# Two graph attention layers on one core: three of eight layer 0 tiles fetched by indirect DMAs, and GpSimd's once-a-batch work in pieces

## The chip, the core and the metric

The kernel runs on one core of a Trainium2 chip. The core has five engines with an instruction stream each: PE (TensorE, matrix products and transposes; PEld is its weight load), DVE (VectorE), ACT (ScalarE), POOL (GpSimd) and SP (SyncE, which here only issues DMAs). The engines wait for each other through semaphores, and each works through its own stream in order. The metric is the device time of one execution, in microseconds; lower is better.

## The reference, cut to what matters

There are B = 16 graphs ("batches") of N = 1024 nodes with D = 64 numbers each. `adj` is a 1024 x 1024 matrix of zeros and ones, symmetric, with ones on the diagonal; a row has about nine ones.

```python
# layer 0: attention with 8 heads over the neighbours
scores = einsum('bmhd,bnhd->bhmn', q, k) * scale + edge_bias[edges]
scores = where(edges > 0, leaky_relu(scores, 0.2), -1e9)
out = einsum('bhmn,bnhd->bmhd', softmax(scores), v) @ Wp + bp
x = layernorm(x + out)
# layer 1: one head, additive scores
s = leaky_relu(u[:, :, None, :] + v[:, None, :, :], 0.2)
e = where(adj > 0, einsum('bijf,f->bij', s, a), -9e15)
x = layernorm(x + elu(einsum('bij,bjf->bif', softmax(e), hp)))
```

## The kernel before, in words

The adjacency is sparse, so the kernel never forms all pairs. For every group of 8 neighbouring rows (`GR`) it makes a list of `SLOTS` = 120 columns: 112 places for nodes that some row of the group has an edge to, and the 8 rows themselves. A mask then removes the pairs without an edge.

A batch is cut into 8 tiles (`NT`) of 128 rows, 16 groups each. What happens to a tile of layer 0 is spread over four steps:

- `load` (SP) brings the tile's column numbers (`cb`, 544 KB, the same on all partitions) from a small DRAM tensor `col_d`, and `indicate` (DVE, L475) compares them with the partition's own number in two operations: the result `f` is a matrix of zeros and ones that picks columns.
- `gather` (PE, L499) multiplies `f` with x to bring the 112 node vectors of each group together. To keep float32 precision x is split into three bfloat16 parts (`thirds`, five operations on POOL, once a batch and layer). A tile costs 2 x 26 matmuls, in two halves `hs`; ACT copies each half out of PSUM into `xg` (L505). `own` (POOL, L484) adds the group's own 8 rows.
- `queries` (PE L586, DVE L587), `score` (PE L603, DVE L611 to L620), `exps` (ACT L629), `divide` (DVE L636, then POOL L637, once for each half of the heads), `turn` (eight transposes of `xg`, PE L518, ACT L519, giving `xn` with a node on each partition), `turn_weights` (PE L645), `attend` (PE L655), `heads`, `rows`, `residual`.
- At the end of a batch of layer 0, `Norm.scale` (POOL L549 to L552: add, pow, subtract, multiply, on all 8 tiles at once) gives x1. Layer 1 (`project`, `weigh`, `exps`, `attend`, `end`) then takes the same tiles with its own gathers; `own_rows` (POOL L728) makes one of its operands, `sums` (L721, L723) another.

Beside this DVE makes the lists of the next batch (`prepare`: it reads `adj`, packs and sorts; its column numbers are `win`, its row bits `who`), cut by `yield` into 41 pieces (`PIECES`).

The order of all instructions on all engines is written out by hand. One loop runs over steps g; step g takes tile t = g mod 8 of batch b = g div 8. In one step the loop calls the stages of several tiles: `gather` and `queries` of layer 0 tile g, `score` of g-1, `exps`, `divide` and `attend` of g-2, `heads` to `residual` of g-3, and of layer 1 the tiles that lie `LAG` = 12 steps back. Five times a step `Lists.place` puts in pieces of `prepare` (as many as `QUOTA` gives to that step) and at most one piece of a side list (the end of layer 1, the last part of the lists). All steps of layers 0 and 1 are thereby interleaved, so that one engine's wait is another tile's work. Buffers rotate in pools: a tile with `bufs=3` can be written again when its third successor needs it and its last reader is done.

The code leaves indirect DMAs unused: every DMA is issued by SP.

Of the kernel before, what the change touches and what calls it, by code (L numbers as in the profile page):

```python
# [9 lines left out]
F32 = mybir.dt.float32  # L10
# [23 lines left out]
def kernel(  # L34
# [30 lines left out]
    def sub(n):  # L65
        return slice(n * D, n * D + D)
# [172 lines left out]
    root = fst.tile([P, 1], F32, name="root")  # L239
    nc.vector.memset(root, -0.5)  # L240
    setup.close()

# [11 lines left out]
    KEPT = 40  # L254
    PIECES = 41
    MULT = 4
# [24 lines left out]

    started, edges, masks, late = {}, {}, {}, {}

    def start(b):

        xs = dbl.tile([P, NT, D], F32, tag="xs", bufs=3, name=f"xs_{b}")
        dg = sml.tile([P, NT], I32, tag="dg", bufs=2, name=f"dg_{b}")
        diag = adj[b].rearrange("r c -> (r c)")[0 : N * N : N + 1]
        for n in range(2):
            nc.sync.dma_start(xs[sub(n), :, :], by_rows(x[b], n))  # L290
            nc.sync.dma_start(
                dg[sub(n), :], diag[n * 512 : n * 512 + 512].rearrange("(t r) -> r t", r=D)
            )
        ads = {}

        def load(k):
            hs, T = divmod(k, NT)
            if hs < 2:
                ads[k] = dbl.tile([P, 2, SEG], I32, tag="ad", bufs=4, name=f"ad_{b}_{hs}_{T}")
                nc.sync.dma_start(  # L300
                    ads[k], adj[b, ts(T, P), :].rearrange("p (n c) -> p n c", n=2)[:, :, hs * SEG : hs * SEG + SEG]
                )

        for k in range(4):
            load(k)
        started[b] = xs, dg, ads, load

    def prepare(b):

        if b not in started:  # L310
            start(b)
        xs, dg, ads, load = started.pop(b)
        flags = sml.tile([P, 32], F32, tag="flags", bufs=2, name=f"flags_{b}")
# [95 lines left out]
        yield  # L409

        rows_s = per.tile([P, NT, 2 * CAP2], BF16, tag="rows_s", name=f"rows_s_{b}")
        for n in range(2):
            for q in range(NQ):
# [5 lines left out]
                )  # L419
        edges[b] = (xs, col_d)  # L420
        late[b] = (flags, dg, rows_s)

    def finish(b):

        flags, dg, rows_s = late.pop(b)
        mask = dbl.tile([P, NT, SLOTS], BF16, tag="mask", bufs=4, name=f"mask_{b}")
        nc.vector.tensor_scalar(mask[:, :, 0 : 2 * CAP2], rows_s, code, NEG, ALU.not_equal, ALU.mult)
# [17 lines left out]
    def thirds(src, tag, nm):  # L445

        t3 = dbl.tile([P, 3, NT, D], BF16, tag=tag, bufs=3, name=f"{tag}_{nm}")
        rest = src
        less = per.tile([P, NT, D], F32, tag="less", name=f"less_{tag}_{nm}")
        for k in range(3):  # L450
            nc.gpsimd.tensor_copy(t3[:, k, :, :], rest)
            if k < 2:
                nc.gpsimd.tensor_tensor(less, rest, t3[:, k, :, :], ALU.subtract)
                rest = less
        return t3

    class Tiles:


        def load(self, t):  # L460
            nm = f"{self.b}_{self.layer}_{t}"
            self.cb[t] = cb = dbl.tile([P, NSEG, 2, NQ, WIN], BF16, tag="cb", bufs=3, name=f"cb_{nm}")
            nc.sync.dma_start(
                cb.rearrange("p s n q k -> p (s n q k)"),
                self.col_d[t].rearrange("s n q k -> (s n q k)").unsqueeze(0).to_broadcast([P, NSEG * 2 * NQ * WIN]),
            )
# [54 lines left out]
        def begin(self, x_):  # L521

            b = self.b
            px = ps_g.tile([P, 512], F32, tag="g", name=f"px{self.layer}_{b}")
            columns_T(px, x_)
            self.xT = dbl.tile([P, 512], F32, tag=f"xT{self.layer}", name=f"xT{self.layer}_{b}")
            nc.scalar.copy(self.xT, px)
            self.t3 = thirds(x_, "x3", f"{self.layer}_{b}")
            self.f, self.xg, self.xn = {}, {}, {}

    def banks(tag, name):
# [3 lines left out]
    class Norm:  # L535
# [10 lines left out]

        def scale(self, dst, y):
            rs = sml.tile([P, NT], F32, tag="rs", name=f"rs_{self.nm}")
            nc.gpsimd.tensor_tensor(rs, self.mv[:, :, 1], eps.to_broadcast([P, NT]), ALU.add)  # L549
            nc.gpsimd.tensor_tensor(rs, rs, root.to_broadcast([P, NT]), ALU.pow)  # L550
            nc.gpsimd.tensor_tensor(dst, y, self.mv[:, :, 0:1].to_broadcast([P, NT, D]), ALU.subtract)
            nc.gpsimd.tensor_tensor(dst, dst, rs.unsqueeze(2).to_broadcast([P, NT, D]), ALU.mult)  # L552

    class Layer0(Tiles):
        layer = 0

        def __init__(self, b):
            self.b, self.cb, (self.xs, self.col_d) = b, {}, edges[b]
            self.begin(self.xs)
            self.mx = dbl.tile([P, 2, NG // 4], F32, tag="mx", name=f"mx_{b}")  # L560
            self.y = dbl.tile([P, NT, D], F32, tag="y", name=f"y0_{b}")
            self.norm = Norm(f"0_{b}")
            self.qp, self.ls, self.den, self.w = {}, {}, {}, {}

        def constants(self):
# [124 lines left out]
        def residual(self, t):  # L690
            if t % 2 == 0:
                return
            nc.vector.tensor_tensor(self.y[:, t - 1 : t + 1, :], self.pr, self.xs[:, t - 1 : t + 1, :], ALU.add)
            for t_ in (t - 1, t):
                self.norm.look(self.y, t_)

        def end(self):
            x1 = dbl.tile([P, NT, D], F32, tag="x1", name=f"x1_{self.b}")
            self.norm.scale(x1, self.y)

# [3 lines left out]
            nc.vector.tensor_tensor(bad, bad, low, ALU.max)  # L704
            return x1

    class Layer1(Tiles):
        layer = 1

        def __init__(self, b, x1):  # L710
            self.b, self.cb, self.x1, (_, self.col_d) = b, {}, x1, edges[b]
            self.begin(x1)
# [4 lines left out]
        def sums(self):  # L717
            pu = ps_g.tile([P, NT, D], F32, tag="g", name=f"pu_{self.b}")
            for t in range(NT):
                for n in range(2):  # L720
                    nc.tensor.matmul(pu[sub(n), t, :], self.xT[:, ts(t, D)], w1h[:, n, :], start=True, stop=True)  # L721
            self.u = dbl.tile([P, NT, D], F32, tag="u", name=f"u_{self.b}")
            nc.vector.tensor_tensor(self.u, pu, rows_b[:, 0:1, :].to_broadcast([P, NT, D]), ALU.add)  # L723
# [85 lines left out]
        def end(self):  # L809
# [12 lines left out]
            norm = Norm(f"1_{b}")  # L822
            for t in range(0, NT, 2):
                norm.look(y, t)
                norm.look(y, t + 1)
                yield
            norm.scale(o, y)
            yield
            for n in range(2):
# [7 lines left out]
    PLACES = 5  # L837
    QUOTA = (3, 3, 5, 6, 6, 6, 6, 6)
    l0, l1 = {}, {}
# [6 lines left out]
    class Lists:  # L846


        def __init__(self):
# [6 lines left out]
            self.done, self.part, self.side = 0, None, []  # L856

        def place(self, g, k):
            b, t = divmod(g + AHEAD, NT)
            due = PIECES * b + sum(QUOTA[:t]) + QUOTA[t] * (k + 1) // PLACES  # L860
            last = k == PLACES - 1
            while self.done < due and self.part != ("keys" if last else "sums"):
                self.part = next(self.work, None)
                self.done += 1
# [7 lines left out]
    with tc.manual_schedule(engines={getattr(mybir.EngineType, e) for e in order}):  # L872
        for _ in prepare(0):
            pass
        for _ in finish(0):
            pass
        l0[0] = Layer0(0)
        l0[0].constants()
        l0[0].load(0)
# [3 lines left out]
        for g in range(NT * B + LAG + 7):  # L883
            u = g - LAG
            b, t = divmod(g, NT)
            if t == 0 and 0 < b < B:
                lists.side.append(finish(b))
            lists.place(g, 0)
            at(l0, g - 2, "exps", 0, range(4))
            at(l0, g - 1, "score", lambda: at(l0, g - 2, "divide", 0))  # L890
            if (g - 1) // NT not in l0:
                at(l0, g - 2, "divide", 0)
            at(l0, g - 2, "exps", 1, range(2))
            at(l0, g, "gather", 0)
            at(l0, g - 3, "heads")
            at(l0, g, "gather", 1)
            at(l0, g - 2, "exps", 1, range(2, 4))
            back = ps_z.tile([P, 3, D], F32, tag="e", name=f"back_{g}") if g > 3 else None
            at(l1, u - 3, "rows", back)
            at(l0, g - 3, "rows", back)  # L900
            at(l0, g, "queries")
            at(l1, u - 3, "residual")
            at(l0, g - 3, "residual")
            if t == 6 and b - 2 in l1:
                lists.side.append(l1[b - 2].end())
            at(l0, g - 2, "divide", 1)
            at(l1, u - 1, "project")
            lists.place(g, 1)
            at(l1, u, "gather", 0)
            at(l0, g - 1, "turn")  # L910
            lists.place(g, 2)
            at(l1, u - 1, "weigh")
            at(l1, u - 1, "exps")
            at(l0, g + 1, "indicate")
            at(l0, g + 2, "load")
            at(l1, u, "gather", 1)
            if t == 2 and b - 1 in l0:
# [19 lines left out]
            if t == 3 and b - 1 in l1:  # L937
                l1[b - 1].sums()
            if t == NT - AHEAD and b + 1 < B:
                l0[b + 1] = Layer0(b + 1)  # L940
                l0[b + 1].load(0)
# [415 lines left out]
```

## Time and profile before

| | us |
|---|---|
| median of three timed runs | 2500.33 (2499.95 to 2503.71) |
| the profiled execution | 2508.74 |
| its span in the profile | 2506.8 |
| busy: PE, DVE, ACT, POOL | 2308.1, 2012.1, 1445.2, 912.9 |
| one batch in the middle (1210.40 to 1356.03) | 145.63 |
| granted clock, mean of the span | 0.988 |

A profile page gives, for each engine, the time in which it worked on some instruction. Groups of instructions are named by line, engine, operation, the tile written and the tiles read, then the shapes, the number, the busy time and the mean of one in ns, and the idle time ahead of them with what ended it. Matmuls overlap in the array, so the busy time of a group is less than number times mean. A table of stretches gives the length and each engine's busy time with its number of instructions, the granted clock, the share of the DMA engines and GB/s. The timeline merges neighbouring instructions of a kind into one row: start, duration, engine, line.

### The profile page before, as it was taken

The numbers are of one execution on the slowest core, as the hardware profiler recorded it, in microseconds if no ns is written. First come the engines' busy times: TensorE is split into PE (matmuls) and PEld (weight loads), VectorE is DVE, ScalarE is ACT, GpSimd is POOL, SyncE is SP. The second block draws the span as 40 slices with busy tenths as digits, with TensorE's granted clock in tenths as the row PEclk, the third lists the DMA queues.
The fourth block names the chain that finished last, engine by engine and source line by source line (L and its number), as shares of the span: only waits on it lengthen the run. The fifth ranks groups of instructions, "written<-read, shape, count | busy, mean of one in ns | idle before, by whom it ended". The sixth has DMA issues, their size and how long they took to land. (4 is left out here: it accounts for less than half of the span.)

```text
span 2506.8 us, 110853 instructions
## 1 busy us (share of the span) xinstructions
PE 2308.1 (92%) x48706; PEld 1957.7 (78%) x48706; DVE 2012.1 (80%) x5237; ACT 1445.2 (58%) x4401; POOL 912.9 (36%) x1106
## 2 busy tenths in 40 slices
PE   5387999999999999999999999999999999999986
PEld 3376788878788887878788787888878888888864
DVE  6687879888888988888898888889888888876642
ACT  0154656656565665656566566656656665666743
POOL 1133333434334343433434343342434434243331
PEclk9998999999999999999999999999999999999998
DMA  3412332423233242323324232332423233221210
GB/s 102 122 59 89 104 103 78 133 77 116 73 102 108 78 133 80 114 73 107 103 78 133 84 109 75 106 103 78 133 86 108 81 100 106 62 92 57 66 52 18
DMA packets 190543, 230.66 MB, mean 92 GB/s; under 512 B 91492, under 2 KB 157092, under 8 KB 190052
## 3 DMA queue, kind: packets, MB, share of 16 engines
q1 hardware_dynamic: 190052, 223.49, 28.3%
q8 instruction: 384, 6.29, 1.0%
q14 instruction: 107, 0.88, 0.1%
HBM read 218.23 MB, written 5.21 MB: 89 GB/s over the span
## 5 line engine op out<-in xcount | busy, mean ns | idle before, releaser
L499 PE MATMUL pg<-f,x 128*64 128x272 bf16 (+2 forms) x13312 | 804.5, 272 | 37.4 <-DVE f L475 34.5
L499 PEld LDWEIGHTS <-x 128*64 128x64 bf16 x13312 | 662.0, 109 | 115.5 <-issue 70.4
L637 POOL TENSOR_TENSOR ls<-ls,den 128x480 f32<-128x480 f32 x256 | 285.8, 1117 | 921.1 <-DVE den L636 912.6
L475 DVE TENSOR_SCALAR f<-cb,jrow 128x2176 bf16<-128x2176 bf16 x512 | 491.6, 1001 | 0.3 <-DMA cb<-col_d 0.3
L505 ACT COPY xg<-pg 128x448 f32<-128x448 f32 x512 | 271.5, 530 | 356.1 <-PE pg L499 355.1
L629 ACT ACTIVATE ls<-ls,mx 128x120 f32<-128x120 f32 x1024 | 391.2, 386 | 4.8 <-DVE mx L620 4.8
L519 ACT COPY xn<-pt 120x512 f32<-120x512 f32 x512 | 277.3, 597 | 11.8 <-PE pt L518 7.1
L751 ACT ACTIVATE r<-pz 128x480 f32<-128x480 f32 x256 | 132.1, 568 | 247.0 <-PE pz L746 247.0
L518 PE MATMUL pt<-ident,xg 128*120 128x128 f32 x2048 | 273.9, 276 | 0.0
L484 POOL COPY xg<-xT 128x64 f32<-128x64 f32 x256 | 107.2, 426 | 387.9 <-PE pt L518 345.4
L518 PEld LDWEIGHTS pt<-ident,xg 128*120 128x120 f32 x2048 | 224.0, 137 | 27.3 <-issue 24.8
L752 DVE SCALAR_TENSOR_TENSOR r<-pz,r 128x480 f32<-128x480 f32 x256 | 155.4, 649 | 50.6 <-ACT r L751 50.6
L629 ACT ACTIVATION_READ_ACCUMULATOR ls<-ls,mx 128x1 f32 x1024 | 194.8, 190 | 0.0
L619 DVE SCALAR_TENSOR_TENSOR ls<-sc 128x480 f32<-128x480 f32 x256 | 191.5, 748 | 0.0
L620 DVE TENSOR_REDUCE mx<-ls 128x4 f32<-128x480 f32 x256 | 167.2, 653 | 8.8
L611 DVE TENSOR_TENSOR sc<-s,rowc 128x480 f32<-128x480 f32 x256 | 155.1, 647 | 22.7 <-PE s L603 21.0
L746 PEld LDWEIGHTS pz<-rw,ub 64*64 64x64 f32 x4096 | 122.6, 133 | 63.9 <-issue 58.5
L655 PE MATMUL z<-w,xn 120*64 120x64 f32 x4096 | 159.2, 227 | 4.4 <-ACT w L647 4.4
L587 DVE TENSOR_TENSOR qp<-pq,qb 128x512 f32<-128x512 f32 x128 | 87.9, 686 | 90.0 <-PE pq L586 89.8
L655 PEld LDWEIGHTS z<-w,xn 120*64 120x64 f32 x4096 | 138.4, 139 | 27.7 <-ACT w L647 19.4
L645 PE MATMUL pp<-ident,ls 128*120 128x128 f32 x1024 | 142.0, 280 | 19.3 <-POOL ls L637 16.6
L740 PE MATMUL pz<-xg,w2d 64*64 64x480 f32 x1024 | 140.4, 588 | 17.1 <-DVE sc L611 17.1
(212 smaller groups left out, 3881.1 us busy)
## 6 DMA issues: line engine op xcount, KB each, us to landing
cb<-col_d SPq DMA_DIRECT2D x256, 544.0 KB
ad<-in_adj_dram SPq DMA_DIRECT2D x256, 256.0 KB
xs<-in_x_dram SPq DMA_DIRECT2D x32, 128.0 KB
rows_s<-slot_d SPq DMA_DIRECT2D x256, 14.0 KB
out_dram<-o SPq DMA_DIRECT2D x32, 128.0 KB
col_d<-col SPq DMA_DIRECT2D x128, 4.2 KB
dg<-in_adj_dram SPq DMA_DIRECT2D x32, 2.0 KB
slot_d<-slot SPq DMA_DIRECT2D x16, 28.0 KB
```

The source lines that it names most:

```text
L475: nc.vector.tensor_scalar(fj.rearrange("p s n q k -> p (s n q k)"), cb.rearrange("p s n q k -> p (s n q k)"), jrow[:, j : j + 1], None, AL ...
L499: nc.tensor.matmul(pg[sub(n), :, FIRST * a_ + lo : FIRST * a_ + to], self.t3[:, k, 4 * hs + 2 * a_ + j, :], f[j][:, 2 * hs + a_, n, :, lo:to],
L505: nc.scalar.copy(dst, pg)
L518: nc.tensor.transpose(pt[:, q, :], xg[:, 4 * m + q, :], ident)
L519: nc.scalar.copy(self.xn[t][:, ts(m, 4), :], pt)
L611: nc.vector.tensor_tensor(sc, both[n], self.rowc[:, n, ts_].unsqueeze(2).to_broadcast([P, 4, SLOTS]), ALU.add)
L619: nc.vector.scalar_tensor_tensor(ls, scs[n], SLOPE, scs[n], ALU.mult, ALU.max)
L620: nc.vector.tensor_reduce(self.mx[:, n, ts_], ls, XX, ALU.max, negate=True)
L629: nc.scalar.activation(ls[:, q, :], ls[:, q, :], AF.Exp, bias=neg[:, q : q + 1], accum_out=den[:, q : q + 1])
L637: nc.gpsimd.tensor_tensor(ls, ls, den.unsqueeze(2).to_broadcast([P, 4, SLOTS]), ALU.mult)
L655: nc.tensor.matmul(zz[sub(n), q, :], xn[:, q, sub(n)], w_[n][:, q // 2, sub(q % 2)], start=True, stop=True)
L752: nc.vector.scalar_tensor_tensor(r, pz[n], SLOPE / (1.0 - SLOPE), r, ALU.mult, ALU.add)
```

## The change

For tiles 2, 5 and 7 of every batch of layer 0, the 120 node vectors of each group are fetched from DRAM by indirect DMAs issued by POOL. `prepare` makes their row numbers (`at_d`: one column of 120 numbers for each group; number 0 is an empty place), `start` makes a copy of x in DRAM in the groups' numbering (`table`). One DMA brings one group (120 rows of 256 bytes, a row on each partition) into `xf`; a tile takes 16, a batch 48. They arrive with a node on each partition, which is what `attend` reads as `xn`; for `xg` the tile is transposed on PE by eight transposes in `gather`, and `turn` does nothing for it. Such a tile has no `load`, `indicate` or `own`. `place` issues one or two fetches each time, two steps ahead of the batch that they are for.

POOL's once-a-batch work is cut up: `thirds` yields after each operation, and the norms of both layers work on two tiles at a time, in place for layer 0 (`x1` is now `y`). The next batch's `Layer0` is made at step 4 in place of 6. Within a step that has a fetched tile the order differs: both halves of its `gather` first, `queries` ahead of `heads`, the second half's last exponentials and the `rows` after the layer 1 gather. In those steps and in the ones after them (`soon`) layer 1's second gather half stands ahead of `weigh`. In the norms the four operations are as before, on [P, 2] and [P, 2, D]. The pieces are now 43, at most two a place, with 7 as the last two entries of `QUOTA`; some pools have one buffer less or more.

```diff
+    own_at = fst.tile([P, GR], F32, name="own_at")
...
+    seg_at = fst.tile([P, N // SEG], F32, name="seg_at")
...
-    PIECES = 41
+    PIECES = 43
...
     def start(b):
         xs = dbl.tile([P, NT, D], F32, tag="xs", bufs=3, name=f"xs_{b}")
+        table = dram.tile([N + 1, D], F32, tag="table", bufs=3, name=f"table_{b}")
+        nc.sync.dma_start(table[0:1, :], x[b, 0:1, :])
...
         for n in range(2):
             nc.sync.dma_start(xs[sub(n), :, :], by_rows(x[b], n))
+            nc.sync.dma_start(
+                table[1 : N + 1, :].rearrange("(t n r) d -> n t r d", n=2, r=D)[n],
+                x[b, n * 512 : n * 512 + 512, :].rearrange("(t r) d -> t r d", r=D),
+            )
...
     def prepare(b):
...
+        tb = per.tile([P, NSEG, WIN], F32, tag="tb", name=f"tb_{b}")
+        nc.vector.tensor_tensor(tb, seg_at.unsqueeze(2).to_broadcast([P, NSEG, WIN]), win, ALU.subtract)
+        nc.vector.scalar_tensor_tensor(tb, who, 0.5, tb, ALU.is_ge, ALU.mult)
+        tv = tb.rearrange("p (s a) k -> p s a k", a=2)
+        at_s = per.tile([P, SLOTS], F32, tag="at_s", name=f"at_s_{b}")
+        av = at_s[:, 0 : 2 * CAP2].rearrange("p (s k) -> p s k", k=CAP2)
+        nc.vector.tensor_copy(av[:, :, 0:FIRST], tv[:, :, 0, 0:FIRST])
+        nc.vector.tensor_tensor(av[:, :, FIRST:WIN], tv[:, :, 0, FIRST:WIN], tv[:, :, 1, 0:SHARE], ALU.max)
+        nc.vector.tensor_copy(av[:, :, WIN:CAP2], tv[:, :, 1, SHARE:WIN])
+        nc.vector.tensor_copy(at_s[:, 2 * CAP2 : SLOTS], own_at)
+        yield
...
+        yield "sums"
+        pi = ps_z.tile([SLOTS, P], F32, tag="z", name=f"pi_{b}")
+        nc.tensor.transpose(pi, at_s, ident)
+        at_d = dbl.tile([SLOTS, P], I32, tag="at_d", name=f"at_d_{b}")
+        nc.vector.tensor_scalar(at_d, pi, 0.0, float(N), ALU.max, ALU.min)
+        edges[b] = (col_d, table, at_d)
...
     def thirds(src, tag, nm):
-        for k in range(3):
-            nc.gpsimd.tensor_copy(t3[:, k, :, :], rest)
-            if k < 2:
-                nc.gpsimd.tensor_tensor(less, rest, t3[:, k, :, :], ALU.subtract)
-                rest = less
-        return t3
+        def parts(rest):
+            for k in range(3):
+                nc.gpsimd.tensor_copy(t3[:, k, :, :], rest)
+                yield
+                if k < 2:
+                    nc.gpsimd.tensor_tensor(less, rest, t3[:, k, :, :], ALU.subtract)
+                    rest = less
+                    yield
+        return t3, parts(src)
...
-            self.xT = dbl.tile([P, 512], F32, tag=f"xT{self.layer}", name=f"xT{self.layer}_{b}")
+            self.xT = dbl.tile([P, 512], F32, tag=f"xT{self.layer}", bufs=2 - self.layer, name=f"xT{self.layer}_{b}")
...
-            self.t3 = thirds(x_, "x3", f"{self.layer}_{b}")
+            self.t3, parts = thirds(x_, "x3", f"{self.layer}_{b}")
+            lists.side.insert(0, parts)
...
-        def scale(self, dst, y):
+        def scale(self, dst, y, t):
+            two = slice(t - 1, t + 1)
+            for t_ in (t - 1, t):
+                self.look(y, t_)
...
+    def fetch(b, t, k):
+        _, table, rows_at = edges[b]
+        if k == 0:
+            fetched[b, t] = dbl.tile([SLOTS, NQ, P], F32, tag="xf", bufs=3, name=f"xf_{b}_{t}")
+        n, q = divmod(k, NQ)
+        g = D * n + NQ * t + q
+        nc.gpsimd.indirect_dma_start(
+            out=fetched[b, t][:, q, sub(n)], out_offset=None, in_=table[:, :],
+            in_offset=bass.IndirectOffsetOnAxis(ap=rows_at[:, g : g + 1], axis=0),
+        )
...
     class Layer0(Tiles):
+        def gather(self, t, hs):
+            if t not in FETCHED:
+                return super().gather(t, hs)
+            nm = f"{self.b}_{t}"
+            if hs == 0:
+                self.xn[t] = fetched.pop((self.b, t))
+                self.xg[t] = dbl.tile([P, NQ, SLOTS], F32, tag="xg0", bufs=2, name=f"xgf_{nm}")
+            pt = ps_p.tile([P, 4, SLOTS], F32, tag="p", name=f"ptf_{nm}_{hs}")
+            for q in range(4):
+                nc.tensor.transpose(pt[:, q, :], self.xn[t][:, 4 * hs + q, :], ident[0:SLOTS, 0:SLOTS])
+            nc.scalar.copy(self.xg[t][:, ts(hs, 4), :], pt)
...
         def residual(self, t):
...
-            for t_ in (t - 1, t):
-                self.norm.look(self.y, t_)
+            self.norm.scale(self.y, self.y, t)
...
-            self.u = dbl.tile([P, NT, D], F32, tag="u", name=f"u_{self.b}")
+            self.u = dbl.tile([P, NT, D], F32, tag="u", bufs=1, name=f"u_{self.b}")
...
-    QUOTA = (3, 3, 5, 6, 6, 6, 6, 6)
+    QUOTA = (3, 3, 5, 6, 6, 6, 7, 7)
+    FETCHED = (2, 5, 7)
...
+        def fetches(self, g, k):
+            b, t = divmod(g + AHEAD, NT)
+            i, todo = PLACES * t + k, 2 * NQ * len(FETCHED)
+            for j in range(todo * i // (PLACES * NT), todo * (i + 1) // (PLACES * NT)):
+                if b < B:
+                    fetch(b, FETCHED[j // (2 * NQ)], j % (2 * NQ))
         def place(self, g, k):
+            self.fetches(g, k)
...
-            while self.done < due and self.part != ("keys" if last else "sums"):
+            end = self.done + 2 if (t, k) != (NT - 1, PLACES - 1) else due
+            while self.done < min(due, end) and self.part != ("keys" if last else "sums"):
...
+        for k in range(2 * PLACES):
+            lists.fetches(k // PLACES - AHEAD, k % PLACES)
         l0[0] = Layer0(0)
+        for _ in lists.side.pop():
+            pass
...
+            if t in FETCHED:
+                at(l0, g, "gather", 0)
+                at(l0, g, "gather", 1)
+                at(l0, g - 2, "exps", 1, range(2))
+                at(l1, u - 3, "rows", back)
+                at(l0, g, "queries")
+                at(l0, g - 3, "heads")
...
+            if t in FETCHED:
+                lists.place(g, 1)
+                at(l1, u, "gather", 0)
+                at(l0, g - 2, "exps", 1, range(2, 4))
+                at(l0, g - 3, "rows", back)
...
+            soon = t in FETCHED or (g - 1) % NT in FETCHED
+            if soon:
+                at(l1, u, "gather", 1)
...
+            if t == 4 and b + 1 < B:
+                l0[b + 1] = Layer0(b + 1)
             if t == NT - AHEAD and b + 1 < B:
-                l0[b + 1] = Layer0(b + 1)
                 l0[b + 1].load(0)
```

## The prediction

> **What bounds the kernel now.** I read the page's busy times first, then the stretch between successive query additions (DVE L587), which cuts one batch into its eight steps, then the timeline inside two steps.
>
> ```profile
> span 2506.8 us, 110853 instructions
> PE 2308.1 (92%) x48706; PEld 1957.7 (78%) x48706; DVE 2012.1 (80%) x5237; ACT 1445.2 (58%) x4401; POOL 912.9 (36%) x1106
> ```
>
> PE is the busiest engine and POOL the idlest. The table by step (start:end, length, then PE, PEld, DVE, ACT and POOL busy, clock, DMA share) says the same of one batch:
>
> ```profile
> 1227.64:1247.03 19.39, 18.24 (x377) 15.04 (x373) 13.03 (x34) 11.48 (x35) 5.14 (x7) 1.00 0.21 70
> 1247.03:1268.87 21.84, 19.91 (x423) 16.92 (x425) 20.71 (x54) 11.77 (x37) 12.79 (x14) 1.00 0.16 53
> 1286.41:1302.71 16.30, 16.30 (x346) 13.94 (x350) 15.16 (x38) 10.87 (x34) 3.71 (x5) 1.00 0.20 73
> 1318.92:1337.63 18.71, 18.19 (x407) 15.67 (x409) 16.61 (x39) 11.77 (x36) 11.22 (x14) 1.00 0.46 140
> 1210.40:1356.03 145.63, 140.41 (x3036) 119.96 (x3040) 124.94 (x314) 90.22 (x276) 56.85 (x68) 1.00 0.31 99
> ```
>
> A batch takes 145.63 us; PE works 140.41 of it and stands 5.2. The second row is the exception: there DVE has 20.71 of 21.84 us, and POOL its longest burst. These rows are the ends of tiles 1, 2, 4 and 6 with the starts of the next. DMA engines are busy a third of the time and bound nothing.
>
> **What is removed.** A fetched tile has no gather of 52 matmuls (L499) and no two indicator rows on DVE (L475).
>
> ```profile
> 1215.22 1.58 PE L499 MATMUL pg<-f,x 128*64 128x272 bf16 x26
> 1216.73 1.09 PE L645 MATMUL pp<-ident,ls 128*120 128x128 f32 x8
> L475 DVE TENSOR_SCALAR f<-cb,jrow 128x2176 bf16<-128x2176 bf16 x512 | 491.6, 1001 | 0.3 <-DMA cb<-col_d 0.3
> ```
>
> Half a gather keeps PE from 1215.22 to 1216.73, 1.51 us, so a tile 3.02 us and a batch, with three tiles, 9.06 us. The eight transposes of turn (L518) are not saved: a fetched tile needs eight in the other direction, of the same size but for 120 columns in place of 128; I cost that at nothing. DVE loses 6 x 1.0 = 6.0 us a batch. ACT loses two copies a tile (L505, 530 ns; the other two stay), POOL three small copies (L484, 426 ns), SP three loads of 544 KB; none of these is on the path. PE gets one transpose a batch (pi), 0.29 us by L780's 285 ns. DVE gets seven small operations (tb, at_s, at_d), about 7 x 0.23 = 1.6 us by L390 to L406. Both removals of tile 2 lie in the first row above, of tile 5 in the third, of tile 7 in the fourth; the second row gains nothing. With the same 5.2 us of standing, a batch would be 145.63 - 9.06 + 0.29 = 136.9 us.
>
> **What is added on POOL.** A tile needs 16 indirect DMAs of 120 rows, so a batch 48, six a step. The trace has no such instruction. Lowest row: an ordinary issue on SP, about 0.6 us (L300, two in 1.27). Highest: POOL's dearest operation, 1862 ns (L550, pow). I take 1.2, the middle, since POOL's full-width operations (L637, 1117 ns) lie there too. That is 57.6 us, with 28.8 and 89.4 as ends.
>
> The layer norms go from two calls of four operations a batch to eight calls on a quarter of the data. A call was 0.20 + 1.69 + 1.05 + 1.25 = 4.2 us. Now the pow has 2 elements in place of 8: at least 0.42 and at most 1.69, I take 0.57 (0.2 fixed, the rest in proportion). The two wide ones go to 128x128, for which L327 has 0.54 us. A call is 1.85, eight are 14.8 against 8.4: +6.4 us (ends +5 and +15). Thirds is the same five operations, put in pieces. POOL outside the DMAs is then 56.85 + 6.4 - 1.3 = 62 us, and in all 62 + 57.6 = 119.6 of 136.9 us, 87%. It still fits; what of it is late is seen below.
>
> **What the added POOL work does to DVE.** The same trace shows POOL and DVE disturbing each other. POOL works without a pause from 1250.26 to 1261.65, and DVE meanwhile does this:
>
> ```profile
> 1250.54 1.68 POOL L550 TENSOR_TENSOR rs<-rs,root 128x8 f32<-128x8 f32 x1
> 1260.66 0.99 POOL L451 CAST x<-less_x 128x512 bf16<-128x512 f32 x1
> 1252.41 0.93 DVE L367 SCALAR_TENSOR_TENSOR kb<-left,c 128x32 f32<-128x32 int32 x1
> 1253.45 2.24 DVE L475 TENSOR_SCALAR f<-cb,jrow 128x2176 bf16<-128x2176 bf16 x2
> 1257.63 1.02 DVE L364 TENSOR_SCALAR left<-left 128x32 int32<-128x32 int32 x1
> 1259.48 2.74 DVE L475 TENSOR_SCALAR f<-cb,jrow 128x2176 bf16<-128x2176 bf16 x2
> 1273.05 1.48 DVE L475 TENSOR_SCALAR f<-cb,jrow 128x2176 bf16<-128x2176 bf16 x2
> ```
>
> A pair of indicators takes 1.48 us alone and 2.24 and 2.74 beside POOL; operations of 0.19 us take 0.93 and 1.02. The excess in that burst is 0.74 + 0.76 + 0.28 + 0.84 + 0.46 + 1.26 = 4.3 us in 11.4, or 0.38 us of DVE per us of POOL. If an indirect DMA holds DVE up like a cast, 57.6 + 5.1 = 62.7 added us cost DVE 24 us, and DVE has 124.9 - 6.0 + 1.6 + 24 = 144.5: as long as a batch is now. If it holds DVE up not at all, DVE has 120.5 plus 2 for the norms. The truth of an operation that reads no wide tile is likely below half: I take a third for the fetches, 7 us, and the 2 of the norms, hence DVE 130 us, below PE's 136.9 in the sum, but not step by step: the second row keeps its 20.7 us, and the rows where the quotas rise get up to two pieces (about 1 us) more. I add 3.6 us a batch for steps that DVE or a late POOL then ends (ends 0 and 8.7), which makes 140.5.
>
> The Trainium skill, "SBUF — State Buffer", sections "A bandwidth-pool intuition that's wrong (but worth ruling out)" and "Who interferes with whom", speaks against this change: VectorE and GpSimd share one port pair as an exclusive lock, and a DMA whose descriptors GpSimd writes took about 620 ns alone and 3100 ns beside a VectorE copy. By 3.1 us a fetch POOL would need 62 + 149 = 211 us a batch, an estimate of some 3,500 us in all; by 0.62 us it would be hidden. The stretched rows above agree that the two engines exclude each other, but nothing here shows an issue from GpSimd.
>
> **The new waits.** The first fetch of a batch waits for at_d, which DVE writes last in the step before; behind it on POOL stands the first division (L637), needed about 12 us later by PE. Once a batch, perhaps 2 us, hidden. Each later fetch waits for the landing of the eighth before it, over 20 us earlier: nothing. The fetches end over a step before the tile is used (tile 7, the closest: issued up to step 5, used in step 7), so PE does not wait for data. The tables (two DRAM copies and a row a batch) stand on SP's queue before the ad loads; three cb issues go, so the queue is no longer. With one buffer for xT1 and u, ACT's copy and DVE's addition wait for POOL's last reader in the same step: at most one POOL operation, about 1 us a batch, inside the 3.6. The division of the second half (L637) moves later in a fetched step; about 6 us of PE work (project, gather, weigh) still lies between it and its transpose.
>
> **Head.** Before the first gather POOL now runs 12 fetches, which wait for at_d at about 79 us (slots are done at 76.56, plus 2), then the thirds that ran at 53.84: 79 + 14.4 + 4.4 = 98 us against the gather's 94.2. With the tables' traffic about +6 us (0 to +12).
>
> **Sum.** Batch 0 has no layer 1 beside it and PE is not the bound there, so fifteen batches count: 15 x (145.63 - 140.5) = 77 us, less 6: 71. The profiled execution, 2508.74 us (span 2506.8, 1.9 around it), becomes 2438. The three timed runs have a median of 2500.33, 8.4 below; I take the change off that: **about 2430 us**.
>
> **Rivals.** (1) *All of PE's gain stays:* fetches do not disturb DVE. 15 x 8.7 = 131, less 2: 2370 us. For it: DVE's sum falls by 4 us. Against: DVE's 20.71 of 21.84 us. Chance 0.12. (2) *DVE eats the gain:* a fetch disturbs it like a cast, DVE has 144.5 us and a batch 144.5 to 147; 2490 to 2525. Chance 0.14. (3) *POOL becomes the bound* (slower): POOL's 62 + 48c passes today's 145.63 us once a fetch costs c = 1.74 us. At 1.86 it is 151.3 us, 15 x 5.7 + 12 = +97, about 2600 us; each further 0.1 us adds 72. Before that point PE already waits for divisions, since POOL is in order. For it: pow costs 1.86 and every fetch may wait for a 0.78 us indicator. Against: 1.2 is the middle. Chance 0.28. (4) That the gathers don't go is excluded: 2,496 matmuls leave the instruction stream.
>
> **How the numbers follow.** The forecast (2390 to 2470) gets 0.46. A run tells about 0.2%, 5 us, from no change. Faster: 0.46 + 0.12 + a little of (2) = 0.60; same: 0.05 out of (2); slower: 0.28 + the rest of (2) = 0.35. The range begins at 2368, just below rival 1's value, and reaches into rival 3 to 2590, leaving out about 0.04 and 0.14. The forecast's own range is 2390 to 2470.
>
> **What would show it.** Right: L543 with 10,816 matmuls; a batch of 139 to 142 us between query additions; POOL near 85% with fetch spacing of 1.0 to 1.4 us; indicator mean above 1001 ns. Wrong: back-to-back fetches spaced over 1.7 us, PE waiting for POOL's divisions by several us a step, or DVE without idle time in all steps.

## The result, and the profile after

Four runs of the changed kernel have a median of 2854.99 us (2853.9 to 2861.56), against 2500.22 us of the kernel before on the same chip: a ratio of 1.142 (95% interval 1.140 to 1.144). It is slower by about 355 us, and the time lies above the whole predicted range.

The page of the profile after: the span, the busy times, and then four of its costliest groups (busy us, mean ns of one, idle time before them and what ended it), with the pow of the norms.

```profile
span 2852.1 us, 106678 instructions
...
PE 2403.2 (84%) x46226; PEld 1966.1 (69%) x46226; DVE 1944.4 (68%) x5261; ACT 1390.4 (49%) x4305; POOL 1788.3 (63%) x2213
...
L615 POOL DMA_INDIRECT xf<-table,at_d x768 | 822.4, 1071 | 211.7 <-issue 182.0
L543 PE MATMUL pg<-f,x 128*64 128x272 bf16 (+2 forms) x10816 | 699.1, 281 | 24.1 <-issue 21.0
L543 PEld LDWEIGHTS <-x 128*64 128x64 bf16 x10816 | 567.9, 113 | 107.0 <-issue 78.3
...
L519 DVE TENSOR_SCALAR f<-cb,jrow 128x2176 bf16<-128x2176 bf16 x416 | 353.8, 891 | 0.0
...
L598 POOL TENSOR_TENSOR rs<-rs,root 128x2 f32<-128x2 f32 x128 | 109.7, 857 | 10.0
```

PE has 2,480 matmuls fewer than before (46,226 against 48,706) and yet is busy 95 us longer. No engine is full: PE 84%, DVE 68%, POOL 63%. "Issue" on PE is time in which it waited for nothing that the profile shows.

The table by step, between query additions (DVE L684), of one batch; the columns are those of before. The rows answer, in this order, to the four rows of before; then comes the step that grew most, and the batch.

```profile
1421.31:1440.63 19.32, 18.15 (x345) 14.31 (x347) 10.34 (x24) 10.16 (x31) 12.26 (x13) 1.00 0.14 41
1440.63:1463.31 22.68, 19.89 (x373) 16.33 (x373) 19.74 (x63) 12.29 (x39) 12.06 (x16) 0.92 0.37 95
...
1315.27:1334.97 19.70, 18.14 (x355) 14.64 (x359) 14.17 (x38) 10.86 (x32) 13.04 (x16) 1.00 0.06 12
...
1356.31:1373.00 16.69, 15.70 (x307) 13.65 (x309) 12.21 (x34) 9.36 (x29) 13.03 (x18) 0.90 0.47 139
1373.00:1398.97 25.97, 21.99 (x436) 16.99 (x435) 13.62 (x36) 12.31 (x39) 18.73 (x26) 0.93 0.32 99
...
1315.27:1483.45 168.18, 150.26 (x2881) 124.77 (x2885) 120.08 (x315) 86.77 (x270) 111.47 (x137) 0.92 0.31 89
```

A batch takes 168.18 us instead of 145.63. PE stands 17.9 us of it (5.2 before), and its mean clock is 0.92, where every row of before had 1.00. Fewer matmuls make more busy time.

What PE's issue looks like beside fetches, in the timeline inside that longest step (start, length, engine, line, and in brackets the idle time before):

```profile
1391.51 0.30 PE L543 MATMUL pg<-f,x 128*64 128x272 bf16 x1
...
1392.06 0.51 PE L543 MATMUL pg<-f,x 128*64 128x272 bf16 x5 [0.25 <-issue]
...
1392.18 0.98 POOL L615 DMA_INDIRECT xf<-table,at_d  x1 [0.30 <-issue]
...
1392.82 0.54 PE L543 MATMUL pg<-f,x 128*64 128x272 bf16 x6 [0.25 <-issue]
...
1393.55 0.62 PEld L543 LDWEIGHTS <-x 128*64 128x64 bf16 x14 [0.47 <-issue]
1393.56 0.89 PE L543 MATMUL pg<-f,x 128*64 128x96 bf16 x14 [0.20 <-issue]
```

The half gather of 26 matmuls, 1.51 us before, takes from 1391.51 to 1394.45, 2.94 us. The profile shows nothing that it waited for: it is broken by pauses that nothing in the trace accounts for.

The clock shows in four stretches of 2 us, and the timeline of PE, DVE and POOL says what stood:

```profile
1340.00:1342.00 2.00, 0.64 (x6) 0.40 (x4) 2.00 (x4) 0.00 (x0) 1.94 (x3) 1.00 0.12 18
1342.00:1344.00 2.00, 0.87 (x8) 0.87 (x9) 1.97 (x8) 1.37 (x5) 0.00 (x0) 1.00 0.10 9
1344.00:1346.00 2.00, 2.00 (x34) 1.74 (x33) 1.93 (x8) 1.33 (x4) 1.36 (x2) 0.53 0.11 15
1346.00:1348.00 2.00, 2.00 (x40) 1.98 (x37) 1.58 (x3) 0.58 (x1) 1.66 (x2) 0.50 0.48 177
```

```profile
1339.56 1.04 POOL L615 DMA_INDIRECT xf<-table,at_d  x1 [0.19 <-issue]
...
1339.98 1.86 DVE L424 CAST slot<-who 128x44 bf16<-128x44 int32 x1
...
1340.61 1.18 POOL L495 TENSOR_TENSOR less_x<-less_x,x 128x512 f32<-128x512 f32 x1
...
1342.32 0.27 DVE L862 TENSOR_REDUCE m<-e 128x1 f32<-128x120 f32 x1
...
1343.13 0.33 PE L874 MATMUL pt<-ident,e 128*120 128x128 f32 x1 [2.49 <-ACT e L868]
```

A cast of DVE that took 0.17 to 0.22 us in every batch before (L401) lasts 1.86 us, here and in the median of the 16 batches, until POOL's fetch and subtraction are through. The maximum m comes late, ScalarE's e too, PE stands 2.49 us, and from 1344.1 on its clock is halved for 6.8 us. The run's mean clock of 0.935 means 2 x 0.065 x 2852 = 371 us at half clock; before it was 0.988, or 60 us. If PE was the bound in all of it, that is (371 - 60) / 2 = 155 us lost, an upper end.

PE's waits over the whole run (us in total, times, longest):

```profile
PE pt L874 <- ACT e L868: 95.8, 66, 2.9
PE pp L742 <- POOL ls L734: 73.0, 28, 4.3
PE s L700 <- issue: 55.7, 154, 1.2
...
PE pg L543 <- issue: 21.0, 66, 1.3
```

Before, the second was 16.6 us and the other three came to 4.0 us together.

### The profile page after: what moved, and what is told of

Read it like the earlier page. It is cut to its first block, busy times and chain, and to the rows that moved or that the text cites. A ratio compares the mean times of both kernels' runs of the same rounds, so it can differ in the third digit from the quotient of the medians.

```text
span 2852.1 us, 106678 instructions
## 1 busy us (share of the span) xinstructions
PE 2403.2 (84%) x46226; PEld 1966.1 (69%) x46226; DVE 1944.4 (68%) x5261; ACT 1390.4 (49%) x4305; POOL 1788.3 (63%) x2213
## 3 DMA queue, kind: packets, MB, share of 16 engines
q0 software_dynamic: 24576, 23.67, 4.4%
## 4 chain that ended last, share of the span: by engine, by line
PE 59%; DVE 19%; POOL 11%; issue 6%; ACT 3%; another core or an unknown queue 1%; DMA 1%; SPq 0%; ACTq 0%; POOLq 0%; DVEq 0%
PE pg L543 15%; PE s L700 6%; PE z L752 4%; PE pt L562 4%; POOL xf L615 4%; PE pq L683 4%; PE pa L885 3%; PE pz L834 3%; PE pz L840 3%; DVE f L519 3%; PE pp L742 3%; PE po L768 2%; DVE r L846 2%; PE pat L356 2%; POOL ls L734 2%
## 5 line engine op out<-in xcount | busy, mean ns | idle before, releaser
L615 POOL DMA_INDIRECT xf<-table,at_d x768 | 822.4, 1071 | 211.7 <-issue 182.0
L543 PE MATMUL pg<-f,x 128*64 128x272 bf16 (+2 forms) x10816 | 699.1, 281 | 24.1 <-issue 21.0
L543 PEld LDWEIGHTS <-x 128*64 128x64 bf16 x10816 | 567.9, 113 | 107.0 <-issue 78.3
L549 ACT COPY xg<-pg 128x448 f32<-128x448 f32 x416 | 218.7, 532 | 464.1 <-PE pg L543 392.7
L519 DVE TENSOR_SCALAR f<-cb,jrow 128x2176 bf16<-128x2176 bf16 x416 | 353.8, 891 | 0.0
L563 ACT COPY xn<-pt 120x512 f32<-120x512 f32 x416 | 227.1, 596 | 26.7 <-PE pt L562 23.3
L562 PE MATMUL pt<-ident,xg 128*120 128x128 f32 x1664 | 236.4, 287 | 0.7 <-ACT xg L549 0.6
L742 PEld LDWEIGHTS pp<-ident,ls 128*120 128x120 f32 x1024 | 112.2, 141 | 103.7 <-POOL ls L734 81.2
L744 ACT COPY w<-pp 120x512 f32<-120x512 f32 x256 | 140.4, 586 | 85.7 <-PE pp L742 77.1
L885 PE MATMUL pa<-eT,xn 120*64 120x8 f32 x4096 | 153.0, 205 | 16.8 <-issue 12.2
```

The costliest lines, as they stand in the source:

```text
L519: nc.vector.tensor_scalar(fj.rearrange("p s n q k -> p (s n q k)"), cb.rearrange("p s n q k -> p (s n q k)"), jrow[:, j : j + 1], None, AL ...
L543: nc.tensor.matmul(pg[sub(n), :, FIRST * a_ + lo : FIRST * a_ + to], self.t3[:, k, 4 * hs + 2 * a_ + j, :], f[j][:, 2 * hs + a_, n, :, lo:to],
L549: nc.scalar.copy(dst, pg)
L562: nc.tensor.transpose(pt[:, q, :], xg[:, 4 * m + q, :], ident)
L563: nc.scalar.copy(self.xn[t][:, ts(m, 4), :], pt)
L615: nc.gpsimd.indirect_dma_start(out=fetched[b, t][:, q, sub(n)], out_offset=None, in_=table[:, :], in_offset=bass.IndirectOffsetOnAxis(ap=r ...
```

## The experiments

Kernels run together are compared through the kernel before on the same chip, whose median stayed between 2503.28 and 2504.11 us.

**e1: the pieces without fetches.** The first four experiments split the change into its parts.

```diff
-    FETCHED = (2, 5, 7)
+    FETCHED = ()
```

> No tile is fetched and no fetch issued; GpSimd's pieces, the small norms, the early start of the next layer 0 and the tables stay, and the order in a step is that of before. Theory A (PE's own clock: TensorE stands 17.9 us a batch instead of 5.2, and each longer stand halves the granted clock for 3.4 to 10 us; the stands come from the order in the steps with fetched tiles and from late divisions): 2500 within 20 us, clock above 0.98. Rival B (the fetches themselves, by the port or by DMA traffic): also about 2500. Rival C (the pieces and small norms cost): over 2600.

Measured 2509.25 us, ratio 1.002 (1.001 to 1.0029). The pieces, the small norms, the tables and the new yields cost some 6 us together. They are not the cause.

**e2: layer 1's second gather half back in its place.**

```diff
-            soon = t in FETCHED or (g - 1) % NT in FETCHED
+            soon = False
```

> As the changed kernel, but layer 1's second gather half stands behind weigh, exps and load in all steps, as before. Theory A, order: TensorE no longer stands for layer 1's exponential (207 us in all, matmul and weight load counted both, so some 100 us of time) and has half-clock spells less; 2600 to 2750, clock above 0.95. Rival B: 2855 within 40 us, since GpSimd's and the DMAs' work are the same. Rival C: the same 2855.

Measured 2873.83 us, 1.1475 (1.1441 to 1.1509). That order is not the cause; PE's waits move from ScalarE's e (95.8 us in the changed kernel, 47.7 here) to VectorE's r (9.8 and 104.1).

**e3: plain loads in place of the fetches.** Six DMAs a batch from SyncE's queue bring as many rows, but not the neighbours, so the numbers computed are others.

```diff
-        nc.gpsimd.indirect_dma_start(
-            out=fetched[b, t][:, q, sub(n)], out_offset=None, in_=table[:, :], ...
+        if k % NQ == 0:
+            nc.sync.dma_start(fetched[b, t][:, :, sub(k // NQ)], table[1 : 1 + SLOTS * NQ, :]...)
```

> As the changed kernel, but the fetched tiles are filled by six plain DMAs a batch issued by SP, so GpSimd issues none; the rows are contiguous ones of the table and not the neighbours (this part of the computation is changed). Theory A: GpSimd is never late, but the order still lets TensorE stand for layer 1's exponential; 2450 to 2650. Rival B: all of TensorE's 145 us comes out, 2360 to 2420. Rival C: stays over 2750.

Measured 2502.98 us, 0.9999 (0.9987 to 1.001). This splits the result in two questions: the fetches cost some 350 us, and without them the 145 us of removed gathers still don't come out. PE waits 78.0 us for ScalarE's e and 35.2 us for VectorE's r instead.

**e4: the fetches alone.** All tiles are gathered in the order of before; the 768 fetches are issued and nobody reads what they bring.

```diff
-    FETCHED = (2, 5, 7)
+    FETCHED = ()
+    ISSUED = (2, 5, 7)
...
-                    fetch(b, FETCHED[j // (2 * NQ)], j % (2 * NQ))
+                    fetch(b, ISSUED[j // (2 * NQ)], j % (2 * NQ))
```

> All 768 fetches are issued at their places, but nobody reads them; all tiles are gathered and the order in a step is that of before. Theory A: TensorE has its cover back, the fetches only delay some divisions; 2510 to 2620, clock above 0.95. Rival B: over 2800, as in the changed kernel or worse, since nothing of TensorE's work is saved. Rival C: as in the run without fetches.

Measured 2882.61 us, 1.1494 (1.1462 to 1.1525): 373 us over e1, 0.49 us a fetch, with nobody waiting for one. Adding up: 2503 + 6 for the pieces + 373 for the fetches = 2882, and the changed kernel has 2855, so in it the removed gathers and the new order together bring 28 us. The weight loads of the gathers between 600 and 2200 us, in e4 and then in e1, show part of where the 373 us go:

```profile
L543 PEld LDWEIGHTS <-x 128*64 128x64 bf16 x7930 | 406.6, 112 | 96.1 <-issue 67.3
```

```profile
L543 PEld LDWEIGHTS <-x 128*64 128x64 bf16 x9204 | 456.0, 109 | 56.6 <-issue 25.8
```

The instructions are hardly longer (112 against 109 ns), but their unexplained gaps grow from 25.8 to 67.3 us, for fewer of them. Over all its lines PE waits 84.3 us in this stretch for nothing that the profile shows, against 3.0 us in e1. From the start times of the trace: in stretches from 0.2 us before to 1.8 us after the start of a fetch, PE starts 1.46 matmuls per 0.1 us, elsewhere 2.16. (In e8 below, where a power stands at each fetch's place, it is 2.13 and 2.10, so the places are not the reason.) In the median VectorE's indicator takes 781 ns inside these stretches and 777 outside, ScalarE's copy of pg 532 in both. So what the fetches slow there is PE's issue. They are not without effect on VectorE: for the same 5,357 instructions it is busy 2,070.4 us in e4 and 1,987.9 in e1, 82 us more.

**e5 to e8: what about the fetch it is.** All gather everything and issue, unread: every second fetch; fetches of 16 rows; DMAs with fixed addresses; a power of 120 x 2 values in place of each.

```diff
e5 -                if b < B:
   +                if b < B and j % 2 == 0:
e6 -            out=fetched[b, t][:, q, sub(n)], ... ap=rows_at[:, g : g + 1]
   +            out=fetched[b, t][0:16, q, sub(n)], ... ap=rows_at[0:16, g : g + 1]
e7 -        nc.gpsimd.indirect_dma_start(...)
   +        nc.gpsimd.dma_start(fetched[b, t][:, q, sub(n)], table[1 + SLOTS * q : 1 + SLOTS * (q + 1), :])
e8 -        nc.gpsimd.indirect_dma_start(...)
   +        nc.gpsimd.tensor_tensor(fetched[b, t][:, q, n : n + 2], eps..., root..., ALU.pow)
```

> All tiles gathered as before, pieces kept, and every second of the unread fetches left out: 384 instead of 768, at the same places. The pieces alone took 2509 us and 768 unread fetches 2883 us, 0.49 us for each. Theory A (each fetch by itself slows TensorE's instruction issue for about a microsecond): half the surcharge, 2680 to 2710 us, and the time in which TensorE waits for nothing that the profile shows is halved too, from 84 to about 42 us in the 1600 us from 600 to 2200. Theory B (it is GpSimd's fullness: fetches hold the divisions and pieces back only where they pile up): far less than half, under 2600 us.

> The 768 unread fetches again, but each of 16 rows instead of 120. Theory A1 (the cost comes with the descriptors and packets of the rows): it shrinks with the rows, below 2600 us, and the instruction itself gets shorter than its 1.07 us. Theory A2 (the cost comes with each indirect DMA as an instruction, whatever its size): 2850 to 2890 us, as with 120 rows.

> In place of each unread fetch GpSimd starts a DMA with fixed addresses: 120 rows of 256 bytes that lie one after another in the table, into the same place of the same tile, 768 times. If descriptors that GpSimd's own software writes are the cost, whether or not the rows are looked up: 2800 to 2890 us. If it is the looking up, or the instruction that does it: under 2560 us. The same 768 transfers in 96 larger ones from SyncE, together with three tiles that were not gathered, took 2503 us.

> In place of each unread fetch GpSimd works out a power of 120 x 2 values (about 0.86 us by the row of the pow in the norms), with no DMA: GpSimd is about as busy as with the fetches. If a busy GpSimd is the cost (divisions that come late, VectorE held): above 2750 us, most of the 374 us. If it is the DMA, or the writing of its descriptors: 2505 to 2560 us, and TensorE's waits for nothing that the profile shows stay at about 3 us between 600 and 2200 us.

Measured: e5 2608.93 us (1.0419, 1.0402 to 1.0437); e6 2983.01 (1.1928, 1.1905 to 1.1951); e7 2567.46 (1.026, 1.0243 to 1.0277); e8 2499.66 (0.9984, 0.9973 to 0.9995). The lines of L615 in e6, e7 and e8:

```profile
L615 POOL DMA_INDIRECT xf<-table,at_d x768 | 722.6, 941 | 200.3 <-issue 155.6
```

```profile
L615 POOL DMA_DIRECT2D xf<-table x768 | 467.8, 612 | 10.2 <-issue 9.6
```

```profile
L615 POOL TENSOR_TENSOR xf<-eps,root 120x2 f32<-120x2 f32 x768 | 598.7, 824 | 0.0
```

And the 1600 us from 600 to 2200 (PE, PEld, DVE, ACT, POOL busy, clock) of e8 and of e4:

```profile
600.00:2200.00 1600.00, 1559.77 (x33754) 1334.13 (x33752) 1357.33 (x3553) 998.33 (x3062) 1089.52 (x1557) 1.00 0.34 105
```

```profile
600.00:2200.00 1600.00, 1465.88 (x28978) 1209.45 (x28980) 1231.52 (x3068) 855.54 (x2630) 1081.52 (x1330) 0.96 0.34 98
```

With POOL equally busy in this stretch (1,090 against 1,082 us), e8 loses nothing (it ends 5 us below the lower of its two ranges): a busy POOL is not the cost. As many DMAs with fixed addresses and the same bytes cost 58 us over e1, 0.08 us each, though they also come from POOL; that is 7 us above the range given for it. Fewer rows help not at all: at 16 rows the cost rises to 474 us, 0.62 us each, above the ranges of both theories. Their instructions are 0.13 us shorter and follow one another more closely (1.24 us instead of 1.37 from start to start, at the quarter of closest ones).

The traffic is settled by the queue that carries POOL's transfers (packets, which are the pieces that the trace records, then MB and share of the DMA engines), first of e4 and then of e7:

```profile
q0 software_dynamic: 24576, 23.67, 4.7%
q0 software_dynamic: 24576, 23.67, 4.6%
```

e7 moves exactly as many packets and bytes as e4 and loses 58 us where e4 loses 373; e6 has the 24,576 packets too, with 3.19 MB, and loses most. So the price belongs to the indirect DMA as an instruction, not to its bytes or packets. e5's expectation failed on both sides: half the fetches cost 100 us, neither half of 373 nor as little as theory B said. PE's waits for nothing that the profile shows are 27.5 us there, a third of e4's and not the half that theory A gave. Its clock is 1.00 between 600 and 2200 us, e4's 0.96.

**e10: the same half, in pairs.**

```diff
-                if b < B and j % 2 == 0:
+                if b < B and j % 4 < 2:
```

> 384 unread fetches as in the kernel with every second one left out (2609 us, 0.26 us for each above the pieces alone), but kept in neighbouring pairs: two issued, two left out. Theory F (fetches that follow each other at once disturb TensorE more than the same number spread out): 2630 to 2700 us. Theory G (only the number counts, and the dearer 768 came from the clock, which drops only above some amount of standing): 2595 to 2620 us.

Measured 2590.72 us, 1.0357 (1.0338 to 1.0375): a little below theory G's values, and F falls. Two in a row are no worse than singles.

Where the pauses lie is seen in the start times. Gaps of 0.4 to 1.0 us between the starts of successive PE instructions, matmuls or weight loads, between 600 and 2200 us, number 27 in e1, 29 in e8, 31 in e10, 82 in e5, 239 in e4 and 350 in e6. The kernel before has 84, nearly all of them waits; without those that a semaphore ended there are 16 before, 3 in e1, 8 in e8, 5 in e7, 7 in e10, 69 in e5, 196 in e4 and 280 in e6. In e4 a fetch has such an unexplained gap within 1.5 us of its start in 1% of cases if it starts over 2.2 us after the last one and at most 30 packets of SyncE's transfers start beside it in that time; in 43% if it follows sooner; in 27% if more of them start; in 50% if both hold. Most fetches have it in nearly every batch or in nearly none. But e10's pairs have hardly any (2% of the close ones), where 72% of e5's close ones do. So closeness and other transfers raise the odds and do not settle it. Nor is it a late delivery of instructions, which come by two DMA queues of their own: a packet of these lands within 13% of e4's unexplained pauses, and would within 11% if the pauses lay anywhere.

e10's 82 us are mostly waits instead: PE stands 7.8 us a batch (e1 4.1), and its batch is 150.2 us against 144.8. VectorE is busy 61 us longer there than in e1, and 56 us longer in e7, which has as few pauses; that the rest of the price comes by way of VectorE is likely but was not isolated. What decides a pause stays open, as does why 768 fetches cost more than twice 384: the clock (mean 0.949 in e4, 0.985 in e1) accounts for at most (294 - 75) / 2 = 110 of the 373 us.

**e9: plain loads in the order of before.** e3 with the body of the step as it was; rows that are not the neighbours, as there.

```diff
-            if t in FETCHED:
-                at(l0, g, "gather", 0)
-                at(l0, g, "gather", 1)
...
+            at(l0, g - 2, "exps", 1, range(2))
+            at(l0, g, "gather", 0)
+            at(l0, g - 3, "heads")
+            at(l0, g, "gather", 1)
```

> The kernel with plain loads from SyncE in place of the fetches (its data are not the wanted rows; it took 2503 us, none of the 145 us of gathering came out), now with the steps in the order of before: score, gather half, heads, gather half, and so on, for fetched tiles too. Theory D (the new order of three steps in eight made the waits for ScalarE's e and VectorE's r, about 113 us in that kernel): 2370 to 2430 us, most of the gain comes out. Theory E (the gathers were what TensorE did while layer 1's chain of score, r, e and weights ran its latencies; without them some wait is there in any order): 2480 to 2520 us, and the waits only move.

Measured 2492.18 us, 0.9954 (0.994 to 0.9967): theory E. The clock is back (0.981 for the run), 17 us come out against e1, and the rest turned into waits of PE:

```profile
PE pt L873 <- ACT e L867: 49.5, 41, 1.7
PE e L859 <- DVE r L845: 47.2, 69, 1.9
```

By batch (mean of ten in the middle): e1 144.8 us with PE standing 4.1, e9 144.0 with 10.4. PE's own time falls by 7.0 us, its standing grows by 6.3.

**e11: one tile only,** spread over the batch, in the order of before.

```diff
-    FETCHED = (2, 5, 7)
+    FETCHED = (7,)
```

> The smallest dose of the change that works: tile 7 alone is fetched (256 fetches, spread over the batch), the others are gathered, steps in the order of before. Theory H (a spread fetch costs 0.26 us of the kernel, a tile has 16 of them, and its gather is worth 3.02 us of TensorE at most): 256 x 0.26 = 67 us lost, at most 16 x 3.02 = 48 us won, from the 2509 us of the pieces alone: 2525 to 2580 us, slower than before. Theory I (a few spread fetches are harmless, and the change only overdid it): under 2480 us.

Measured 2520.4 us, 1.0076 (1.0058 to 1.0094): the sign of H, 5 us below its values. Even the smallest dose, with real rows, is 0.8% slower than the kernel before.

**e12: the pieces without the tables,** all tiles gathered; the row numbers and their transpose go too, and `PIECES` and `QUOTA` are those of before.

```diff
-        table = dram.tile([N + 1, D], F32, tag="table", bufs=3, name=f"table_{b}")
-        tb = per.tile([P, NSEG, WIN], F32, tag="tb", name=f"tb_{b}")
...
-        nc.tensor.transpose(pi, at_s, ident)
-        nc.vector.tensor_scalar(at_d, pi, 0.0, float(N), ALU.max, ALU.min)
-    PIECES = 43
+    PIECES = 41
```

> The pieces of GpSimd's work and the norms by pairs of tiles, with no fetch and without what only fetches need: the copy of x into a table, the row numbers, their transpose and their constants. With these the pieces took 2509 us, although a batch in the middle was shorter (144.75 us against 145.71 of before, by the times of the query rows), so that the loss lies at the head and tail. Theory J (the tables hold up the head and the early batches): 2480 to 2498 us, faster than before. Theory K (the pieces themselves cost at the head and tail): 2500 to 2510 us.

Measured 2496.59 us, 0.9975 (0.9964 to 0.9986): theory J. This is a little faster than the kernel before; the tables and row numbers cost some 11 us (0.45%).

**e13 and e14: is VectorE the new bound?** e9 and e1 with one indicator a tile, used in place of both, so that other numbers are computed.

```diff
-            for j in range(2):
+            for j in range(1):
...
-                self.f[t].append(fj)
+                self.f[t] += [fj, fj]
```

> The kernel with plain loads in the order of before (2492 us; 10.4 us of standing a batch), with one indicator f made a tile where the kernel makes two, and used for both (its data are wrong already): VectorE does 13 x 0.9 = 11.7 us less a batch, 187 us in all; TensorE's work is the same. Theory L (with the gathers gone VectorE became the engine that sets the pace): 2300 to 2420 us. Theory M (the standing is latency of layer 1's chain from score to weights, which TensorE's order cannot fill): 2460 to 2495 us.

> The control for the run before: all tiles gathered, no fetch, pieces as in the changed kernel (2509 us, TensorE stands 4.1 us a batch), with one f a tile where the kernel makes two: VectorE does 16 x 0.9 = 14.4 us less a batch. TensorE is the bound there by every theory, so at most its standing is to be had: 2430 to 2510 us.

Measured 2433.02 us (0.9719, 0.9705 to 0.9734) and 2484.07 us (0.9921, 0.9906 to 0.9936). In e13 VectorE is busy 178 us less than in e9 (1,771.9 against 1,949.6), which brings 59 us, a time between the ranges of L and M; the control, with 187 us less than e1, gets 25. With light VectorE the removed gathers are worth 51 us, with the full one 17. PE's wait for VectorE's r fell from 33.6 to 18.1 us between 600 and 2200 us, that for ScalarE's e stayed (41.3 and 41.8). So VectorE is part of what holds the gain back, and the chain through e may be another; how the rest divides was not settled. Even so, most of the 145 us stay away.

## Why the prediction was wrong

*The steps that failed.* First, "What is added on POOL" and what followed from it: the fetches were priced as POOL's time and as VectorE's delay, and nowhere as something that PE pays. 57.6 us a batch were found to "still fit". e8 shows that they do fit, as POOL's time; e4 shows that the fetches alone cost 373 us, in PE's pauses, in waits and in the clock; their shares are known only as the upper ends above, and what causes a pause stays open. Second, "With the same 5.2 us of standing, a batch would be ... 136.9 us": the standing is not the same. e9, with no fetch at all, stands 10.4 us and gains 0.7 us a batch on e1, not 8.8; PE's own time falls by 7.0. Third, no term for the clock, since every row of before had 1.00; at most 155 us lie there.

*POOL's time.* Right: 1.2 us a fetch was taken, 1.07 busy and 1.3 to 1.4 from start to start were measured; 119.6 us a batch were expected, 111.5 found. A call of the norms was put at 1.85 us with a pow of 0.57; the pow took 0.857, the call 1.99.

*VectorE's delay.* About right in size: 7 us a batch were taken for the fetches, and e4 against e1 shows 82 / 16 = 5.2. The sign that was named for it failed: the indicator's mean was to rise above 1001 ns and is 891, because it was down to 879 in e1, with the pieces alone, and the unread fetches raise it to 924 in e4. (The burst from which the rate was read has one idle stretch of 0.40 us, before 1255.48, and the sum leaves out an operation of 0.77 us at 1256.04.) The delay was priced as VectorE's time; what costs is where it falls, as with the cast of 1.86 us, which holds up the chain to PE.

*The new waits.* The division's wait was put inside 3.6 us a batch; PE's waits for it are 73.0 us in all, 4.6 a batch (1.0 before). Right in kind, somewhat low. But they are not what decides: e2 has 24.6 us of them and is no faster, and e4, with every fetch and the order of before, has 13.6.

*The head.* +6 was taken for it; e12 against e1 puts the tables and row numbers at about 11 us for the whole run.

*The rivals.* Rival 3 had the sign, slower, but not by its mechanism: it needed over 1.74 us a fetch and a full POOL. Rivals 1 and 2 fall with PE's standing.

*The Trainium skill.* "SBUF — State Buffer", section "A bandwidth-pool intuition that's wrong (but worth ruling out)", spoke of about 3100 ns for a DMA issued by GpSimd beside a VectorE copy, against 620 alone. Here the indirect ones took POOL 1018 ns in the median of 768 and 1951 at most, the plain ones of e7 554 and 1091. "TensorE: Matmul & The Clock Gate", Part 1, section "What's actually happening", has the clock halved after an idle window of about 3.4 us (3413 ns, free-running). The lengths agree: the changed kernel's clock record has 28 spells of half clock between 600 and 2200 us (before none), of 3.4, 6.8 or 10.2 us. The condition is milder here, if an idle window means one without work: in the 3.4 us ahead of each spell PE was busy 25 to 76% of the time, and the longest time between two starts of PE was 0.6 to 2.8 us, in 13 of the 28 cases under 1.2 us.

## What to carry to other kernels

Before an engine's idle time is filled with a new kind of instruction, issue it unread beside the untouched work: one such run priced here what no row of the old trace could, and it showed that the victim was another engine. And work taken from an engine that is 96% busy is not saved time: once the filler was gone, the waits under it came up, 6.3 of 7.0 us a batch. A clock that has always been full is a resource with a price of its own: here a stand of 2.49 us was followed by 6.8 us at half clock, so that a wait can be paid for twice.

## What the runs showed of the hardware

An indirect DMA of 120 rows of 256 bytes takes 1.07 us of POOL, of 16 rows 0.94: nearly all of it does not depend on the rows. One with fixed addresses takes 0.61. With 768 of them in the run, an unread indirect DMA made this kernel 0.49 us longer (0.62 with 16 rows), and 0.21 to 0.26 at half the number; one with fixed addresses and the same packets 0.08, a power on POOL in its place nothing. The pauses were found in PE's issue; VectorE's busy time grew by 82 us.
